# A two-layer graph network: another order of its beginning, and of all engines' queues

## The chip, the cores and the metric

The kernel runs on one core of a Trainium2 chip. The metric is the device time in microseconds; the number before is the median of ten runs. Five engines work side by side, each through its own queue of instructions: PE (matrix products), DVE (vector), ACT (scalar functions), POOL, and SP, which here only issues transfers. ACT and POOL issue transfers as well. An instruction waits on semaphores for what it needs, and what stands behind it in the same queue waits with it.

## The reference

x and adj are 64 graphs of 256 nodes with 256 features and a 256 x 256 adjacency, in float32.

```python
# layer 0
deg = adj.sum(-1); deg = where(deg != 0, deg, 1)
a = deg^-0.5 * adj * deg^-0.5 + max(alpha, 1e-10) * I
x = layernorm(x + (a @ x) @ W.T + b)
# layer 1, on the x of layer 0
xc = x transposed                                # channels x nodes
h = relu(bn1(conv1(xc)))                         # 1 tap
x_conv = relu(bn2(conv2(h)) + xc) transposed     # 17 taps, padding 8
s = x @ w_se.T + b_se                            # 3 columns
A = exp(-|s_n - s_m|^2) * adj
x_nmp = A @ relu(x @ w_msg.T + b_msg)
y = GRUCell(input [x_conv, x_nmp], hidden x)
out = layernorm(x + y)
```

## The kernel before, in words

The 64 graphs go through in four groups (q) of Q = 16. The convolution with 17 taps (conv2) is done in the frequency domain: every graph is cut into 8 tiles of 32 nodes, each tile with its margins (48 points) is transformed by a product with a small table (fwd, L442), the products over channels are done for each frequency with transformed weights (p_k, L497), and DVE carries out the inverse transform (real_transform, complex_begin, complex_end; L599 to L708). So a group has three stages: layer0 and layer1 for each graph, up to the transform (graphs, L866); the products and the inverse (products, complex_end); and the gates of the recurrent cell with the last layer norm (gru, L753). The stages of different groups are interleaved by generators: a stage yields after each piece, and merge, take and the table PLACES say whose piece is traced next (L835 to L877, L950 to L991). In the first group the pieces of weights (L270) stand beside the graphs: they scale the taps, transform them with a second table (dft_w, L283) and store them in DRAM (ud), from where the products read them again.

The queues are not written out by hand. The program is traced in an order, and the framework then simulates it with a model of how long instructions take and puts each engine's instructions into its queue in the order in which the simulation issues them, the earlier traced ahead of the later among those that are ready. The same simulation decides which buffer of a pool a tile gets.

The beginning is what most of the change is about. At L106 to L113 the loads of graphs 0 and 1 are asked for on SP (adj_t, then x_t, each 256 KB), with alpha between them, and the weights of layer 0, conv1 and the messages on ACT. Then come:

- batch_norms (L139): eight vectors are loaded as 16 rows (L144), transposed (L148), turned into a scale and a shift, and spread over all partitions by products of a matrix of ones with diagonals (L165). The scale of bn1 goes into wc1 (L167), its shift into bc1 (L170); that of bn2 is handed to weights.
- layer0 (L325): degrees (L334 by DVE for graphs 0 and 1, L337 by ACT for the others), their inverse roots (dis, L340, POOL), the transposed adjacency (p_adjT, L349; copied by ACT, L350), its two diagonal blocks with alpha added (adjT, L352, DVE), x scaled by dis (x1, L361, ACT) and x plus bias (L362, POOL). Then the first product (p_hT, L369), the second (p_out, L379), the sum (L383) and the layer norm (L294). It yields ahead of the first product, ahead of the second, and at its end.
- tables (L196): a row of cosines is written on one partition by 48 memsets (period, L199). w_row (L216, L217) and fwd_row (L240, L241) are filled by one copy for every frequency, real and imaginary. Both rows go through DRAM: w_row to wd and from there to the 85 partitions of wt (L220 to L224), from which dft_w is made (L231); fwd_row to fm, which POOL fills with zeros first (L210, L242), and from there in six shifted pieces to fwd (L246).
- At L879 to L888 these are traced in the order: vectors, first taps, biases, layer0 of graphs 0 and 1, the rest of the batch norms, the tables, the load of graph 2.

Of the kernel before, what the change touches and what calls it, by code (L numbers as in the profile page):

```python
# [9 lines left out]
F32 = mybir.dt.float32  # L10
# [4 lines left out]
P = 128  # L15
# [5 lines left out]
def bcast_rows(v, n, rows=P):  # L21

    return bass.AP(tensor=v.tensor, offset=v.offset, ap=[[0, rows], [1, n]])
# [3 lines left out]
def kernel(  # L27
# [41 lines left out]

    const = ctx.enter_context(tc.tile_pool(name="const", bufs=1))  # L70
# [18 lines left out]
    def load(g):  # L89
        if g >= B:  # L90
            return
        ain[g] = loads.tile([P, NCH, N], F32, name="adj_t")
        nc.sync.dma_start(ain[g], adj[g].rearrange("(c p) m -> p c m", p=P))
        xin[g] = loads.tile([P, NCH, D], F32, name="x_t")
        nc.sync.dma_start(xin[g], x[g].rearrange("(c p) f -> p c f", p=P))
# [9 lines left out]

    load(0)  # L106
    nc.sync.dma_start(alpha_t, bcast_rows(alpha, 1))
    load(1)
    nc.scalar.dma_start(w0, w0T.rearrange("(k p) o -> p k o", p=P))
    nc.scalar.dma_start(b0_t, bcast_rows(b0, D))  # L110
    nc.scalar.dma_start(wc1[:, :, :D], conv1T.rearrange("(k p) o -> p k o", p=P))
    nc.scalar.dma_start(wc1[:, :, D:], w_seT.rearrange("(k p) o -> p k o", p=P))
    nc.scalar.dma_start(wmsg, w_msgT.rearrange("(k p) o -> p k o", p=P))  # L113
# [4 lines left out]
    neg_half = const.tile([P, 4], F32)  # L118
    nc.vector.memset(neg_half, -0.5)
# [19 lines left out]
    def batch_norms(pool):  # L139


        vectors = pool.tile([16, P], F32, name="bn_in")
        for i, a in enumerate((bn1_g, bn2_g, bn1_b, bn2_b, bn1_m, bn2_m, bn1_v, bn2_v)):
            nc.sync.dma_start(vectors[2 * i : 2 * i + 2], a.rearrange("(c p) -> c p", p=P))  # L144
        scale = pool.tile([P, D], F32, name="scale")
        yield
# [41 lines left out]
    fm_rows = 2 * P + NT  # L188
    fm0 = P - PAD
    fm = dram.tile([fm_rows, FL], F32, name="fm")  # L190
# [5 lines left out]
    def tables(pool):  # L196
        period = pool.tile([1, 25 * FL], F32, name="period")
# [10 lines left out]
        zeros = pool.tile([NT, FL * fm_rows // NT], F32, name="zeros")  # L208
        nc.gpsimd.memset(zeros, 0.0)
        nc.gpsimd.dma_start(fm.rearrange("(p r) f -> p (r f)", p=NT), zeros)  # L210

        for r in range(2):
            nc.vector.memset(w_row[:, :, r, NF], (0.5, 1.0)[r])
        nc.vector.memset(w_row[:, 1::2, 1, NF], 0.0)
        for n, f in enumerate(FREQ):
            nc.vector.tensor_copy(w_row[:, :, 0, n], wave(f, False, TAPS))  # L216
            nc.vector.tensor_copy(w_row[:, :, 1, n], wave(f, True, TAPS))  # L217

        wd = dram.tile([TAPS, 2 * NU], F32, name="wd")
        nc.sync.dma_start(wd.unsqueeze(0), w_row.rearrange("p t h n -> p t (h n)"))  # L220
        wt = pool.tile([KT, 2 * NU], F32, name="wt")
        for c in range(GC):
            nc.sync.dma_start(wt[c * TR : (c + 1) * TR], wd[:TR])
        nc.sync.dma_start(wt[GC * TR :], bcast_rows(wd[TR], 2 * NU, GC))  # L224
# [10 lines left out]

        for r in range(2):
            nc.vector.memset(fwd_row[:, :, 2 * r], 1.0)
        nc.vector.memset(fwd_row[:, 1::2, 2], -1.0)
        for n, f in enumerate(FREQ):
            nc.vector.tensor_copy(fwd_row[:, :, RE[n]], wave(f, False, FL))  # L240
            nc.vector.tensor_copy(fwd_row[:, :, IM[n]], wave(-f, True, FL))  # L241
        nc.sync.dma_start(fm[fm0 : fm0 + FL].unsqueeze(0), fwd_row)  # L242
        for j in range(GT // 2 + 2):

            first = fm0 + PAD - NT * (j - 1)
            nc.sync.dma_start(fwd[:, j, :], fm[first : first + P])  # L246
# [75 lines left out]
    ADJT, DIS, XB, X1, XN, MSG, AT = {}, {}, {}, {}, {}, {}, {}  # L322


    def layer0(g):  # L325
# [7 lines left out]
        if g < 2:  # L333
            nc.vector.tensor_reduce(deg, a_t, AX.X, ALU.add)  # L334
        else:
            for c in range(NCH):
                nc.scalar.activation(adjT[:, c, 0:2, :].rearrange("p n q -> p (n q)"), a_t[:, c, :], AF.Copy, accum_out=deg[:, c : c + 1])  # L337
# [12 lines left out]
        nc.scalar.copy(adjT[:, :, 0:3:2, :], p.rearrange("p c (n q) -> p c n q", q=P))  # L350
        for mc in range(NCH):
            nc.vector.scalar_tensor_tensor(  # L352
                adjT[:, mc, 1, :], ident, adeg[:, mc : mc + 1], adjT[:, mc, 2 * mc, :],
                op0=ALU.mult, op1=ALU.add,
            )
# [4 lines left out]
        for c in range(NCH):  # L360
            nc.scalar.activation(x1[:, c, :], x_t[:, c, :], AF.Copy, scale=dis[:, c : c + 1])  # L361
# [497 lines left out]
    def run(stage):  # L859
        for _ in stage:  # L860
            pass
# [17 lines left out]
    with tc.tile_pool(name="setup", bufs=1) as setup:  # L879
        norms = batch_norms(setup)  # L880
        next(norms)
        load_taps(setup, 0)
        nc.sync.dma_start(bmsg_t, bcast_rows(b_msg, D))
        nc.sync.dma_start(bc1[:, D:], bcast_rows(b_se, NSE))
        run(merge(layer0(0), layer0(1)))
        scale2 = next(norms)
        tables(setup)
        load(2)  # L888

# [155 lines left out]
```

## Time and profile before

| | |
|---|---|
| median of ten runs | 2192.78 us (2190.47 to 2200.57) |
| the profiled execution | 2195.79 us |
| its span, first to last instruction | 2194.0 us |
| granted clock of PE, mean | 0.984 |
| PE idle in the first 60 us | 60 - 35.64 = 24.4 us |
| PE idle from 400 to 520 us | 120 - 98.15 = 21.9 us |
| DMA, mean over the span | 139 GB/s |

The 40 slices of the span, in tenths of busy time (54.85 us each; PEclk is the clock granted to PE):

```profile
PE   5999989969999997999999998899999999899998
PEld 4878778758888886888888887688888887678887
DVE  5555558875568799655556889855555879987666
ACT  3556533445441122456542122446553112222222
POOL 2444310113321234223222224322231223344442
PEclk9999999979999999999999999999999999999999
DMA  3756656443347644333336654433333654444441
```

A row is one engine, a digit one slice. PE is at 9 in most slices; it is below in the first, and in those where DVE is at 8 or 9 and the stages of two groups meet. A product of 256 columns takes about 0.22 us of PE when they follow each other (24 of p_rz in 5.18 us on the chain), so busy PE is work that the order of the queues can't remove.

### The profile page before, as it was taken

The numbers are of one execution on the slowest core, as the hardware profiler recorded it, in microseconds if no ns is written. First come the engines' busy times: TensorE is split into PE (matmuls) and PEld (weight loads), VectorE is DVE, ScalarE is ACT, GpSimd is POOL, SyncE is SP. The second block draws the span as 40 slices with busy tenths as digits, with TensorE's granted clock in tenths as the row PEclk, the third lists the DMA queues.
The fourth block names the chain that finished last, engine by engine and source line by source line (L and its number), as shares of the span: only waits on it lengthen the run. The fifth ranks groups of instructions, "written<-read, shape, count | busy, mean of one in ns | idle before, by whom it ended". The sixth has DMA issues, their size and how long they took to land. (4 is left out here: it accounts for less than half of the span.)

```text
span 2194.0 us, 28939 instructions
## 1 busy us (share of the span) xinstructions
PE 2067.6 (94%) x9805; PEld 1751.9 (80%) x9805; DVE 1553.6 (71%) x3743; ACT 828.8 (38%) x1838; POOL 664.1 (30%) x641
## 2 busy tenths in 40 slices
PE   5999989969999997999999998899999999899998
PEld 4878778758888886888888887688888887678887
DVE  5555558875568799655556889855555879987666
ACT  3556533445441122456542122446553112222222
POOL 2444310113321234223222224322231223344442
PEclk9999999979999999999999999999999999999999
DMA  3756656443347644333336654433333654444441
GB/s 98 231 187 199 221 164 217 154 140 112 100 114 217 199 118 125 115 101 111 109 108 177 206 159 123 127 106 115 102 97 120 203 163 117 119 120 111 104 113 54
DMA packets 251822, 305.83 MB, mean 139 GB/s; under 512 B 18796, under 2 KB 230336, under 8 KB 251673
## 3 DMA queue, kind: packets, MB, share of 16 engines
q1 hardware_dynamic: 183338, 199.93, 30.0%
q10 hardware_dynamic: 45280, 68.04, 8.8%
q0 software_dynamic: 23056, 36.01, 8.4%
q8 instruction: 78, 1.28, 0.2%
q14 instruction: 70, 0.57, 0.1%
HBM read 200.79 MB, written 103.12 MB: 139 GB/s over the span
## 5 line engine op out<-in xcount | busy, mean ns | idle before, releaser
L767 PE MATMUL p_rz<-wrz,sums 128*128 128x256 f32 x1536 | 356.0, 383 | 19.4 <-DVE gn L809 9.8
L804 PE MATMUL p_n<-wn,inputs 128*128 128x256 f32 x1536 | 351.3, 381 | 16.1 <-DVE first L780 15.7
L767 PEld LDWEIGHTS p_rz<-wrz,sums 128*128 128x128 f32 x1536 | 288.5, 191 | 70.9 <-issue 15.8
L804 PEld LDWEIGHTS p_n<-wn,inputs 128*128 128x128 f32 x1536 | 285.7, 190 | 62.1 <-DVE first L780 18.9
L767 PE MATMUL p_rz<-wrz,inputs 128*128 128x256 f32 x1152 | 272.9, 380 | 2.1 <-ACT inputs L739 1.5
L304 POOL TENSOR_TENSOR ln_rs<-ln_rs,neg_half 128x2 f32<-128x2 f32 x129 | 100.2, 777 | 539.8 <-DVE ln_rs L303 454.1
L767 PEld LDWEIGHTS p_rz<-wrz,inputs 128*128 128x128 f32 x1152 | 216.8, 190 | 33.7 <-ACT inputs L739 3.6
L340 POOL TENSOR_TENSOR dis<-deg,neg_half 128x2 f32<-128x2 f32 x64 | 48.5, 757 | 428.1 <-DVE deg L338 321.7
L816 ACT ACTIVATE nn<-gn 128x256 f32<-128x256 f32 x128 | 53.2, 416 | 325.0 <-DVE gn L813 324.3
L497 PE MATMUL p_k<-u,VM 128*128 128x256 f32 x736 | 175.2, 380 | 0.0
L314 ACT ACTIVATE x_g<-x_g,ln_mr,ln_rs 128x256 f32<-128x256 f32 x128 | 70.0, 593 | 256.4 <-DVE ln_mr L312 256.4
L497 PEld LDWEIGHTS p_k<-u,VM 128*128 128x128 f32 x736 | 138.6, 190 | 19.7 <-DMA u<-ud 0.9
L442 PE MATMUL p_dft<-fwd,h 128*128 128x240 f32 x512 | 121.4, 382 | 24.0 <-ACT h L411 23.1
L407 PE MATMUL p_conv<-wc,xn 128*128 128x259 f32 x512 | 128.6, 394 | 14.4 <-ACT xn L399 13.8
L748 POOL TENSOR_TENSOR sums<-inputs 128x384 f32<-128x384 f32 x64 | 69.4, 1085 | 230.1 <-issue 172.2
L369 PE MATMUL p_hT<-adjT,x 128*128 128x256 f32 x512 | 126.5, 392 | 8.3 <-DVE adjT L352 8.1
L442 PEld LDWEIGHTS p_dft<-fwd,h 128*128 128x128 f32 x512 | 98.0, 196 | 41.0 <-ACT h L411 32.7
L473 PE MATMUL p_nmp<-aT,msg 128*128 128x256 f32 x512 | 123.7, 385 | 2.6 <-DVE aT L468 2.6
L379 PE MATMUL p_out<-w,hT 128*128 128x256 f32 x512 | 124.2, 386 | 1.0 <-ACT hT L374 0.7
L407 PEld LDWEIGHTS p_conv<-wc,xn 128*128 128x128 f32 x512 | 97.5, 194 | 33.9 <-ACT xn L399 18.6
L428 PE MATMUL p_msg<-wmsg,xn 128*128 128x256 f32 x512 | 123.4, 385 | 0.0
L362 POOL TENSOR_TENSOR x_t<-x_t,b_t 128x512 f32<-128x512 f32 x64 | 84.7, 1324 | 128.0 <-ACT x L361 88.4
(153 smaller groups left out, 3845.5 us busy)
## 6 DMA issues: line engine op xcount, KB each, us to landing
u<-ud SPq DMA_DIRECT2D x284, 256.0 KB
xn_d<-xn ACTq DMA_DIRECT2D x64, 512.0 KB
inputs<-xn_d SPq DMA_DIRECT2D x64, 512.0 KB
ud<-u_set POOLq DMA_DIRECT2D x39, 480.0 KB, 6.1
adj_t<-in_adj_dram SPq DMA_DIRECT2D x64, 256.0 KB
x_t<-in_x_dram SPq DMA_DIRECT2D x64, 256.0 KB
x_d<-x ACTq DMA_DIRECT2D x64, 256.0 KB
x_g<-x_d SPq DMA_DIRECT2D x64, 256.0 KB
```

Of the source, the lines that this page charges most:

```text
L304: nc.gpsimd.tensor_tensor(rs[:, : len(chunks)], rs[:, : len(chunks)], neg_half[:, : len(chunks)], op=ALU.pow)
L314: nc.scalar.activation(y[:, c, :], y[:, c, :], AF.Identity, bias=mr[:, c : c + 1], scale=rs[:, c : c + 1])
L362: nc.gpsimd.tensor_tensor(x_t, x_t, b0_t.unsqueeze(1).to_broadcast([P, NCH, D]), op=ALU.add)
L369: nc.tensor.matmul(p[:, k, :], x1[:, mc, k * P : (k + 1) * P], adjT[:, mc, 1 - mc : 3 - mc, :].rearrange("p n q -> p (n q)"), start=mc == ...
L379: nc.tensor.matmul(p[:, c, :], hT[:, k, c * P : (c + 1) * P], w0[:, k, :], start=k == 0, stop=k == DCH - 1)
L407: nc.tensor.matmul(p, x1T[:, k, c * P : (c + 1) * P], wc1[:, k, :], start=k == 0, stop=k == DCH - 1)
L428: nc.tensor.matmul(p[:, c, :], x1T[:, k, c * P : (c + 1) * P], wmsg[:, k, :], start=k == 0, stop=k == DCH - 1)
L442: nc.tensor.matmul(p[:, t0 * FL : t1 * FL], h[:, c, k * P : (k + 1) * P], fwd[:, first : first + t1 - t0, :].rearrange("p t f -> p (t f)") ...
L473: nc.tensor.matmul(p[:, k, :], msg[:, mc, k * P : (k + 1) * P], aT[:, mc].rearrange("p n q -> p (n q)"), start=mc == 0, stop=mc == NCH - 1,)
L497: nc.tensor.matmul(p[:, j * D : (j + 1) * D], v[:, k, :], u[:, k, :], start=k == 0, stop=k == DCH - 1)
L767: nc.tensor.matmul(p[:, j * D : (j + 1) * D], a[:, k], wrz[:, b, k], start=k == 0, stop=k == HALF - 1)
L804: nc.tensor.matmul(p[:, o * D : (o + 1) * D], lhsT, w, start=j == 0, stop=j == len(part) - 1)
```

## The change

The first part rearranges the beginning. The bn vectors become a tile of the constants and their loads are issued ahead of most others, four on ACT and four on SP; alpha is asked for on ACT directly after graph 0; a small ACT copy into bc1 stands ahead of everything else on ACT's engine; the weights' loads move from ACT to SP, apart from w0. The tables are made with fewer copies (one for each frequency pair only for part of the frequencies, the others copied or negated from there in one operation each; w_row is copied from fwd_row) and go from SBUF to SBUF, so that wd, fm and the zeros go away, and fwd is cleared by POOL. `issue_after` puts the instructions of its block behind a named instruction on the same engine. Degrees of graphs 0 and 1 are taken by ACT. The order of tracing becomes: two pieces of layer0, the tables, two pieces, the batch norms, the rest of layer0.

The second part is one line: the whole kernel is put into a block that is scheduled with `schedule_with_timeline_sim=True`, so that the simulation which orders all queues and gives out the buffers uses another model.

```diff
--- before.py
+++ after.py
@@ -67,6 +67,8 @@
     NQ = B // Q
     assert N == 256 and D == 256 and B % Q == 0 and TAPS == FL - NT + 1 and FL == 3 * NT // 2
 
+
+    ctx.enter_context(tc.block(schedule_with_timeline_sim=True))
     const = ctx.enter_context(tc.tile_pool(name="const", bufs=1))
     dram = ctx.enter_context(tc.tile_pool(name="dram", bufs=1, space=bass.MemoryType.DRAM))
 
@@ -103,20 +105,25 @@
     bmsg_t = const.tile([P, D], F32)
     alpha_t = const.tile([P, 1], F32)
 
+    vectors = const.tile([16, P], F32, name="bn_in")
+    neg_half = const.tile([P, 4], F32)
+    nc.vector.memset(neg_half, -0.5)
     load(0)
-    nc.sync.dma_start(alpha_t, bcast_rows(alpha, 1))
+    nc.scalar.dma_start(alpha_t, bcast_rows(alpha, 1))
+
+    nc.scalar.copy(bc1[:, :4], neg_half)
+    for i, a in enumerate((bn1_g, bn2_g, bn1_b, bn2_b, bn1_m, bn2_m, bn1_v, bn2_v)):
+        (nc.sync if i % 2 else nc.scalar).dma_start(vectors[2 * i : 2 * i + 2], a.rearrange("(c p) -> c p", p=P))
+    nc.scalar.dma_start(w0, w0T.rearrange("(k p) o -> p k o", p=P))
     load(1)
-    nc.scalar.dma_start(w0, w0T.rearrange("(k p) o -> p k o", p=P))
-    nc.scalar.dma_start(b0_t, bcast_rows(b0, D))
-    nc.scalar.dma_start(wc1[:, :, :D], conv1T.rearrange("(k p) o -> p k o", p=P))
-    nc.scalar.dma_start(wc1[:, :, D:], w_seT.rearrange("(k p) o -> p k o", p=P))
-    nc.scalar.dma_start(wmsg, w_msgT.rearrange("(k p) o -> p k o", p=P))
+    nc.sync.dma_start(b0_t, bcast_rows(b0, D))
+    nc.sync.dma_start(wc1[:, :, :D], conv1T.rearrange("(k p) o -> p k o", p=P))
+    nc.sync.dma_start(wc1[:, :, D:], w_seT.rearrange("(k p) o -> p k o", p=P))
+    nc.sync.dma_start(bc1[:, D:], bcast_rows(b_se, NSE))
 
 
     ident = const.tile([P, P], F32)
     make_identity(nc, ident)
-    neg_half = const.tile([P, 4], F32)
-    nc.vector.memset(neg_half, -0.5)
     nc.vector.tensor_scalar(alpha_t, alpha_t, MIN_ALPHA, None, op0=ALU.max)
 
 
@@ -139,11 +146,7 @@
     def batch_norms(pool):
 
 
-        vectors = pool.tile([16, P], F32, name="bn_in")
-        for i, a in enumerate((bn1_g, bn2_g, bn1_b, bn2_b, bn1_m, bn2_m, bn1_v, bn2_v)):
-            nc.sync.dma_start(vectors[2 * i : 2 * i + 2], a.rearrange("(c p) -> c p", p=P))
         scale = pool.tile([P, D], F32, name="scale")
-        yield
         p = bank("p_bn")
         nc.tensor.transpose(p[:, :16], vectors, ident[:16, :16])
         cols = pool.tile([P, 4, 4], F32, name="bn")
@@ -185,15 +188,13 @@
     KT = GC * TAPS
     TR = 16
 
-    fm_rows = 2 * P + NT
-    fm0 = P - PAD
-    fm = dram.tile([fm_rows, FL], F32, name="fm")
 
     ud = [dram.tile([NU * GC, GW, D], F32, name=f"ud{i}") for i in range(3)]
     fwd = const.tile([P, GT // 2 + 2, FL], F32)
     DFT_W = {}
 
     def tables(pool):
+
         period = pool.tile([1, 25 * FL], F32, name="period")
         for k in range(FL):
             nc.vector.memset(period[:, k::FL], math.cos(2 * math.pi * k / FL))
@@ -205,23 +206,40 @@
 
         fwd_row = pool.tile([1, FL, FL], F32, name="fwd_row")
         w_row = pool.tile([1, TAPS, 2, NU], F32, name="w_row")
-        zeros = pool.tile([NT, FL * fm_rows // NT], F32, name="zeros")
-        nc.gpsimd.memset(zeros, 0.0)
-        nc.gpsimd.dma_start(fm.rearrange("(p r) f -> p (r f)", p=NT), zeros)
-
+        nc.gpsimd.memset(fwd, 0.0)
         for r in range(2):
-            nc.vector.memset(w_row[:, :, r, NF], (0.5, 1.0)[r])
-        nc.vector.memset(w_row[:, 1::2, 1, NF], 0.0)
+            nc.vector.memset(fwd_row[:, :, 2 * r], 1.0)
+        nc.vector.memset(fwd_row[:, 1::2, 2], -1.0)
         for n, f in enumerate(FREQ):
-            nc.vector.tensor_copy(w_row[:, :, 0, n], wave(f, False, TAPS))
-            nc.vector.tensor_copy(w_row[:, :, 1, n], wave(f, True, TAPS))
-
-        wd = dram.tile([TAPS, 2 * NU], F32, name="wd")
-        nc.sync.dma_start(wd.unsqueeze(0), w_row.rearrange("p t h n -> p t (h n)"))
+
+            if f < 0 or f % 3 == 0:
+                nc.vector.tensor_copy(fwd_row[:, :, RE[n]], wave(f, False, FL))
+                nc.vector.tensor_copy(fwd_row[:, :, IM[n]], wave(-f, True, FL))
+        parts = fwd_row[:, :, 16:].rearrange("p t (h n) -> p t h n", h=2)
+        nc.vector.tensor_copy(parts[:, 0::2, :, :8], parts[:, 0::2, :, 8:])
+        nc.vector.tensor_scalar(parts[:, 1::2, :, :8], parts[:, 1::2, :, 8:], -1.0, None, op0=ALU.mult)
+        with tc.issue_after(DIAGONAL[0]):
+
+            for r in range(2):
+                nc.vector.memset(w_row[:, :, r, NF], (0.5, 1.0)[r])
+            nc.vector.memset(w_row[:, 1::2, 1, NF], 0.0)
+            for n0, n1 in ((0, 1), (1, 2), (2, 3), (3, 7), (7, NF)):
+                nc.vector.tensor_copy(w_row[:, :, 0, n0:n1], fwd_row[:, :TAPS, RE[n0] : RE[n0] + n1 - n0])
+            for n0, n1 in ((0, 1), (1, 2), (2, 3), (3, 7), (7, NF)):
+                nc.vector.tensor_scalar(
+                    w_row[:, :, 1, n0:n1], fwd_row[:, :TAPS, IM[n0] : IM[n0] + n1 - n0], -1.0, None, op0=ALU.mult
+                )
+        for j in range(GT // 2 + 2):
+
+            first = NT * (j - 1) - PAD
+            lo, hi = max(first, 0), min(first + FL, P)
+            nc.sync.dma_start(fwd[lo:hi, j, :], fwd_row[:, lo - first : hi - first])
+
         wt = pool.tile([KT, 2 * NU], F32, name="wt")
+        row = w_row.rearrange("p t h n -> p t (h n)")
         for c in range(GC):
-            nc.sync.dma_start(wt[c * TR : (c + 1) * TR], wd[:TR])
-        nc.sync.dma_start(wt[GC * TR :], bcast_rows(wd[TR], 2 * NU, GC))
+            nc.sync.dma_start(wt[c * TR : (c + 1) * TR], row[:, :TR])
+            nc.sync.dma_start(wt[GC * TR + c : GC * TR + c + 1], row[:, TR])
         mask = pool.tile([KT, GC], F32, name="mask")
         dft_w = DFT_W[0] = pool.tile([KT, 2, NU, GC], F32, name="dft_w")
         nc.vector.tensor_reduce(
@@ -232,18 +250,6 @@
             dft_w.rearrange("p h n c -> p (h n) c"), wt.unsqueeze(2).to_broadcast([KT, 2 * NU, GC]),
             mask.unsqueeze(1).to_broadcast([KT, 2 * NU, GC]),
         )
-
-        for r in range(2):
-            nc.vector.memset(fwd_row[:, :, 2 * r], 1.0)
-        nc.vector.memset(fwd_row[:, 1::2, 2], -1.0)
-        for n, f in enumerate(FREQ):
-            nc.vector.tensor_copy(fwd_row[:, :, RE[n]], wave(f, False, FL))
-            nc.vector.tensor_copy(fwd_row[:, :, IM[n]], wave(-f, True, FL))
-        nc.sync.dma_start(fm[fm0 : fm0 + FL].unsqueeze(0), fwd_row)
-        for j in range(GT // 2 + 2):
-
-            first = fm0 + PAD - NT * (j - 1)
-            nc.sync.dma_start(fwd[:, j, :], fm[first : first + P])
 
     TAPS_OF = {}
 
@@ -319,7 +325,7 @@
     xc_d = [dram.tile([Q, N, D], F32, name=f"xc_d{q}") for q in range(NQ)]
     x1_d = [dram.tile([Q, N, D], F32, name=f"x1_d{q}") for q in range(NQ)]
     xn_d = [dram.tile([P, 2 * DCH, N], F32, name=f"xn_d{g}") for g in range(B)]
-    ADJT, DIS, XB, X1, XN, MSG, AT = {}, {}, {}, {}, {}, {}, {}
+    ADJT, X1, X_SCALED, DIAGONAL = {}, {}, {}, {}
 
 
     def layer0(g):
@@ -330,11 +336,19 @@
         ADJT[g] = adjT
 
         deg = small.tile([P, NCH], F32, name="deg")
-        if g < 2:
-            nc.vector.tensor_reduce(deg, a_t, AX.X, ALU.add)
+        def degrees():
+            for c in range(NCH):
+                nc.scalar.activation(
+                    adjT[:, c, 0:2, :].rearrange("p n q -> p (n q)"), a_t[:, c, :], AF.Copy,
+                    accum_out=deg[:, c : c + 1],
+                )
+
+        if g == 1:
+
+            with tc.issue_after(X_SCALED[0]):
+                degrees()
         else:
-            for c in range(NCH):
-                nc.scalar.activation(adjT[:, c, 0:2, :].rearrange("p n q -> p (n q)"), a_t[:, c, :], AF.Copy, accum_out=deg[:, c : c + 1])
+            degrees()
         nc.vector.scalar_tensor_tensor(deg, deg, 0.0, deg, op0=ALU.is_equal, op1=ALU.add)
         dis = small.tile([P, NCH], F32, name="dis")
         nc.gpsimd.tensor_tensor(dis, deg, neg_half[:, :NCH], op=ALU.pow)
@@ -347,18 +361,19 @@
         for mc in range(NCH):
             for c in range(NCH):
                 nc.tensor.transpose(p[:, mc, c * P : (c + 1) * P], a_t[:, c, mc * P : (mc + 1) * P], ident)
-        nc.scalar.copy(adjT[:, :, 0:3:2, :], p.rearrange("p c (n q) -> p c n q", q=P))
+        copied = nc.scalar.copy(adjT[:, :, 0:3:2, :], p.rearrange("p c (n q) -> p c n q", q=P))
         for mc in range(NCH):
-            nc.vector.scalar_tensor_tensor(
+            DIAGONAL[g] = nc.vector.scalar_tensor_tensor(
                 adjT[:, mc, 1, :], ident, adeg[:, mc : mc + 1], adjT[:, mc, 2 * mc, :],
                 op0=ALU.mult, op1=ALU.add,
-            )
+            ).ins
 
 
         x1 = work.tile([P, NCH, D], F32, name="x1")
         X1[g] = x1
-        for c in range(NCH):
-            nc.scalar.activation(x1[:, c, :], x_t[:, c, :], AF.Copy, scale=dis[:, c : c + 1])
+        with tc.issue_after(copied.ins) if g < 2 else ExitStack():
+            for c in range(NCH):
+                X_SCALED[g] = nc.scalar.activation(x1[:, c, :], x_t[:, c, :], AF.Copy, scale=dis[:, c : c + 1]).ins
         nc.gpsimd.tensor_tensor(x_t, x_t, b0_t.unsqueeze(1).to_broadcast([P, NCH, D]), op=ALU.add)
 
         yield
@@ -877,14 +892,15 @@
             yield from given["other"]
 
     with tc.tile_pool(name="setup", bufs=1) as setup:
-        norms = batch_norms(setup)
-        next(norms)
         load_taps(setup, 0)
+        nc.sync.dma_start(wmsg, w_msgT.rearrange("(k p) o -> p k o", p=P))
         nc.sync.dma_start(bmsg_t, bcast_rows(b_msg, D))
-        nc.sync.dma_start(bc1[:, D:], bcast_rows(b_se, NSE))
-        run(merge(layer0(0), layer0(1)))
-        scale2 = next(norms)
+        firsts = merge(layer0(0), layer0(1))
+        run(take(firsts, 2))
         tables(setup)
+        run(take(firsts, 2))
+        scale2 = next(batch_norms(setup))
+        run(firsts)
         load(2)
 
         def gate_weights():
```

## The prediction

> **What bounds the kernel now.** I read the page's busy time and slices first, then the busy time in twelve stretches cut at the visible dips of PE, then PE's waits of the worst stretches, and last the order of time of the beginning. Busy time, by engine:
>
> ```profile
> PE 2067.6 (94%) x9805; PEld 1751.9 (80%) x9805; DVE 1553.6 (71%) x3743; ACT 828.8 (38%) x1838; POOL 664.1 (30%) x641
> ```
>
> PE lacks 2194.0 - 2067.6 = 126.4 us, and that is all that an order of instructions can win, since no matmul is taken away. Where it lies (us from, to; length; busy time of each engine; granted clock; DMA share and rate):
>
> ```profile
> 0.00:60.00 60.00, 35.64 (x142) 28.29 (x143) 35.39 (x217) 18.32 (x40) 15.95 (x26) 0.94 0.35 99
> 60.00:200.00 140.00, 136.09 (x660) 112.16 (x660) 77.04 (x198) 84.66 (x196) 62.04 (x59) 0.99 0.68 212
> 200.00:300.00 100.00, 89.89 (x418) 71.97 (x416) 46.58 (x130) 53.51 (x127) 34.48 (x33) 0.95 0.55 177
> 400.00:520.00 120.00, 98.15 (x449) 77.91 (x448) 93.46 (x262) 57.97 (x131) 27.92 (x27) 0.90 0.41 124
> 800.00:910.00 110.00, 97.24 (x437) 80.80 (x436) 100.25 (x236) 36.75 (x80) 41.55 (x37) 0.95 0.43 122
> 910.00:1290.00 380.00, 376.48 (x1828) 322.21 (x1827) 244.83 (x587) 157.83 (x353) 99.69 (x100) 1.00 0.46 138
> ```
>
> The reader is to see three kinds of stage: the beginning (24.4 us idle of 60), stages in which PE is full (60 to 200, 910 to 1290), and crossings in which DVE is nearly full and PE starves (21.9 us idle in 400 to 520, 12.8 in 800 to 910; two more, 1290 to 1420 and 1790 to 1960, lack 15.6 and 18.1; the end after 1960 lacks 9.3). What PE waited for in the first 60 us (total, times, longest):
>
> ```profile
> PE p_adjT L349 <- DMA adj_t<-in_adj_dram: 8.6, 2, 4.4
> PE p_hT L369 <- DVE adjT L352: 7.6, 1, 7.6
> PE p_norm L165 <- DVE bn L156: 4.3, 1, 4.3
> PE p_u L283 <- DVE dft_w L231: 1.7, 1, 1.7
> ```
>
> In the order of time (start, duration) these waits come from the queues:
>
> ```profile
> 8.84 0.51 ACT L361 ACTIVATE x<-x_t,dis 128x256 f32<-128x256 f32 x1
> 12.16 3.08 DVE L216 COPY w_row<-period 1x17 f32<-1x17 f32 x1
> 12.72 2.49 POOL L362 TENSOR_TENSOR x_t<-x_t,b_t 128x512 f32<-128x512 f32 x2
> 18.00 0.59 DVE L352 SCALAR_TENSOR_TENSOR adjT<-ident,adeg,adjT 128x128 f32<-128x128 f32 x2
> 18.39 6.12 PE L369 MATMUL p_hT<-adjT,x 128*128 128x256 f32 x16 [7.62 <-DVE adjT L352]
> 38.11 2.02 PE L407 MATMUL p_conv<-wc,xn 128*128 128x259 f32 x8 [0.67 <-ACT xn L399]
> 41.38 0.41 DVE L231 TENSOR_TENSOR dft_w<-wt,mask 85x240 f32<-85x240 f32 x1
> ```
>
> The last input of p_hT other than the diagonal is x1, there at 8.84 + 0.51 = 9.35; the diagonal (L352) came at 18.00 because DVE's queue had the 46 table copies ahead of it.
>
> [...] after a wait of 9.56 us at 469.01 eight p_dft take 3.57 us, against 1.62 warm. [...] the 3.08 us copy above, against a median of 0.16, lies over POOL's additions. [...] here it is 1.28 us, at 6.67, behind x0's arrival and in front of the first x1. [...] the store of zeros took 2.6 us to land.
>
> **The change, part by part: the beginning.**
> (1) The w_row work is put behind the diagonal of graph 0, and fwd_row behind the first pieces of layer0. p_hT can start near 9.7 instead of 18.39: 8.7 us off the chain. Nothing else holds it: adeg was ready at 8.68, and alpha, which landed for 8.26, is now first in ACT's queue.
> (2) The table load goes ahead of the data (the small ACT copy into bc1). Degrees of graphs 0 and 1 move to ACT, about 4 x 0.6 us by the later L337 rows (0.41 + 0.19), graph 1's behind x1 of graph 0. I set both together at 0: 1.28 us won, 1.2 us of degrees of graph 0 added on the chain. Bounds -1.3 and +1.2.
> (3) Batch norms ahead of out0. Before, PE did only norms from 28.89 to 36.09, while x1 of graph 0 was normalised at 29.33 + 1.09 = 30.42 and waited for its transposes until 36.09: 5.6 us off the chain. It is not free: the same work now stands ahead of out0. On DVE it is some 16 instructions: nine small at 0.16, six diagonals at 0.28 and the 0.68 and 0.42 of wc and bc, 4.2 us, plus a pow of 1.01 and turns between PE and DVE for a pair of diagonal buffers, 0.5 each. Part lies beside layer0 of graph 1, whose adjacency landed only at 9.65. Cost: 2 at least, 8 at most; I take 4, about the DVE work.
> (4) Tables. DVE before: 48 memsets 2.3 us, 46 copies of w_row at a pitch of 0.083 = 3.8 plus the 3.1 caught by POOL, 46 of fwd_row at 0.115 = 5.3. After: the memsets, 30 copies at 0.115 and two of 384 elements (0.41 by the dft_w row, 240 elements), w_row in 10 operations at 0.16 to 0.41 (272 elements are the largest): 2.3 + 3.5 + 0.8 + 2.5 = 9.1, against 14.5. The DRAM legs (w_row to wd to wt, fwd_row to fm to fwd) and the zeros go; dft_w at 41.4 was ended by that leg and held p_u 1.7 us. I count the 1.7 and leave the DVE time as slack. On SP, 6 fwd and 10 wt issues (0.4 each, 6.4 us) now wait for the rows, where load(2) stands behind; it was at 38.69, so even issued at 25 it is earlier. The eight vector issues at 0.53 stand ahead of load(1) on SP and of w0 on ACT, four on each: graph 1's adjacency up to 2 us later, beside graph 0's work.
> Sum: 8.7 + 5.6 + 1.7 - 4 = 12.0 us earlier at p_conv and p_u. From 60 to 200 PE is full, so the gain is carried on. A single-partition source for the SBUF-to-SBUF tables has no row in this trace: at worst it takes 6 us of the gain (as much as the old path with its two hops seems to have cost), at best nothing. Range of this part: -16 to -5.
>
> **The change, part by part: the queues.** The whole kernel is put into a block whose instructions are listed by simulating with another model. Instructions, sizes and counts stay; the order in each queue and the buffer that a tile gets may change. No view shows the new order. What bounds it: waits of PE after 60 us that lie outside the DVE-full crossings come to 3.9 + 10.1 + 0.9 + 3.5 + 3.5 + 2.5 = 24.4 us (the stretches 60 to 400, 520 to 800, 910 to 1290, 1420 to 1790). Those a better order could take; the 68 us in the crossings it can hardly take, DVE being full there. On the other side a poorer order can open new stalls, up to two as below (44 us). I take -4, a sixth of the 24.4: p_dft behind h, and p_n behind first, are waits of the kind where something ready stands behind something that isn't. [...]
>
> Against the profiled execution (2195.79 us, 1.8 of it outside the span): 2195.8 - 12 - 4 = 2179.8. The median shown is 2192.78, 3.0 lower: 2176.8, so 2177.
>
> **Rivals.**
> A, the forecast: 2177; own range 2160 to 2188.
> B, the beginning's gain is absorbed: something later than the first graphs sets the time, for instance the hand-over at 255 to 300, where the setup pool closes and u, stored by POOL, is read back. For it: 10.1 us idle there. Against it: PE is full from 60 to 255, and the weights' stores follow PE. Time: 2192.
> C, slower: the new order opens another cold stall at a crossing. Price, from the one at 459 to 490: waits of 9.6 + 5.3 us, then eight p_dft 3.57 for 1.62, eight p_hT 3.78 for 1.89, p_dist and p_out likewise, 5.6 us to 485.5 and some 7 in all: 22 us. One such: 2181 (the beginning alone) + 22 = 2203; two: 2225. It decides from the point where PE's idle time outside the first 60 us grows by more than the beginning's 12. For it: three other crossings with DVE full, whose stalls today are short (3.9 us at most), and turns of the stages written out in the program (PLACES and the takes), which don't move when the queues do. Against it: PE's priorities remain those of the program.
> D, the other model gives the same order: 2181, only the beginning shows.
>
> **How the numbers follow.** A 0.54, D 0.05, B 0.11, C 0.30. This kernel can be told from no change at about 0.2% (4.4 us: 2188.4 to 2197.2). A's tail gives 0.01 to that: faster 0.58, same 0.12, slower 0.30. The range takes A, D, B and one stall of C: 2155 (a queue gain of 24 with the 12) to 2215 (one stall and the beginning at its least, or a stall and a half). Outside lie C's two stalls, 0.13, and 0.05 below. Faster and slower both hold much; A's own range is given above.
>
> **What would show it.** Right: p_hT near 10 and p_conv near 26 instead of 38.11; PE idle in the first 60 us near 12; no wait of dft_w on wt; p_rows and p_dft at the first crossing as long as before. (1) is wrong if L352 of graph 0 still ends after 12. (3) is wrong if out0 stands idle behind the norms for over 8 us. The forecast is wrong if PE's idle time in the four crossings leaves 68 us by more than 10, to either side, or the clock there falls.

## The result, and the profile after

| | before | after |
|---|---|---|
| median | 2193.8 us (beside the runs of after) | 2298.87 us (2292.54 to 2303.79) |
| ratio | | 1.0472, 95% interval 1.0459 to 1.0485 |
| span of the profiled execution | 2194.0 us | 2293.3 us |
| granted clock of PE, mean | 0.984 | 0.965 |

The changed kernel is slower by 4.7%, some 104 us. The forecast, 2177 us with a range up to 2215, was wrong in its sign. The page of after, busy time by engine:

```profile
PE 2108.2 (92%) x9805; PEld 1782.9 (78%) x9805; DVE 1566.3 (68%) x3691; ACT 833.4 (36%) x1847; POOL 668.8 (29%) x640
```

PE does the same 9805 matmuls, yet is busy for 2108.2 us, 40.6 more than before, and idle for 2293.3 - 2108.2 = 185.1, 58.7 more: together the 99.3 us between the spans. So two fifths of the loss are matmuls at a lower clock (0.965 in the mean, for 0.984), and the rest is waiting. Where, by the same stretches as before (us from, to; length; busy time and instructions of PE, PEld, DVE, ACT, POOL; clock; DMA share and rate):

```profile
0.00:60.00 60.00, 43.23 (x152) 32.89 (x153) 33.99 (x163) 22.62 (x50) 22.30 (x31) 0.83 0.67 191
60.00:200.00 140.00, 121.00 (x546) 98.46 (x546) 77.01 (x157) 70.33 (x159) 64.29 (x61) 0.93 0.70 218
400.00:520.00 120.00, 95.83 (x432) 76.24 (x431) 91.07 (x256) 55.46 (x124) 25.10 (x24) 0.93 0.43 130
800.00:910.00 110.00, 89.92 (x370) 74.62 (x369) 108.20 (x230) 20.16 (x41) 40.39 (x28) 0.91 0.37 108
910.00:1290.00 380.00, 363.07 (x1747) 306.81 (x1746) 221.72 (x573) 168.98 (x383) 98.50 (x104) 0.98 0.41 120
1420.00:1790.00 370.00, 346.70 (x1648) 292.45 (x1647) 218.28 (x578) 166.43 (x372) 96.47 (x100) 0.98 0.34 103
```

The last of these looked so before:

```profile
1420.00:1790.00 370.00, 367.47 (x1785) 313.74 (x1784) 234.40 (x570) 155.09 (x345) 93.07 (x93) 1.00 0.44 131
```

The beginning does a little more work in its 60 us than before (152 matmuls for 142), at a lower clock (0.83 for 0.94). For its length, the largest loss is from 60 to 200, a stage in which PE had been full: 136.09 us busy before, 121.00 now, with 546 matmuls done for 660. From 910 to 1290 and from 1420 to 1790, full as well before, 13 and 21 us are gone. (The later stretches are shifted by the time already lost, so they show where PE starves, not the exact loss of a stage.) PE's waits over the whole run (total, times, longest):

```profile
PE p_conv L422 <- ACT xn L414: 42.1, 40, 6.7
PE p_n L819 <- DVE trz L796: 22.1, 5, 6.6
PE p_n L819 <- DVE first L795: 20.1, 8, 5.7
PE p_u L289 <- DVE taps L281: 11.4, 4, 4.5
...
PE p_dft L457 <- ACT h L426: 6.0, 5, 2.5
```

Before, the longest in total were these:

```profile
PE p_dft L442 <- ACT h L411: 23.1, 10, 9.6
PE p_n L804 <- DVE first L780: 15.7, 13, 2.4
PE p_conv L407 <- ACT xn L399: 13.8, 11, 3.9
```

So the waits of p_conv, of p_n and of p_u grow, and that of p_dft for h gets shorter. From 60 to 200 us two of them make nearly all of PE's idle time (19.0 us, 3.9 before): p_u waits 8.0 us for its taps, and p_conv 10.9 us for xn. The first, in the order of time (start, duration):

```profile
83.63 7.15 PE L289 MATMUL p_u<-taps,dft_w 85*120 85x256 f32 x16 [4.46 <-DVE taps L281]
90.57 2.67 PE L457 MATMUL p_dft<-fwd,h 128*128 128x240 f32 x8
```

The pieces of the weights now come earlier and in clumps of 16 products, and PE waits for DVE, which has to scale their taps; then the matmuls are slow (16 of p_u take 3.62 us elsewhere, eight of p_dft 1.78). The second, late in the first group:

```profile
119.95 3.69 PE L289 MATMUL p_u<-taps,dft_w 85*120 85x256 f32 x16 [1.85 <-DVE taps L281]
...
138.24 0.60 PE L413 MATMUL p_x1T<-ident,x 128*128 128x128 f32 x4
145.53 3.82 PE L422 MATMUL p_conv<-wc,xn 128*128 128x259 f32 x8 [6.69 <-ACT xn L414]
149.14 1.06 PE L363 MATMUL p_adjT<-ident,adj_t 128*128 128x128 f32 x4
```

Before, the same place looks so:

```profile
142.71 0.60 PE L398 MATMUL p_x1T<-ident,x 128*128 128x128 f32 x4
143.15 1.89 PE L283 MATMUL p_u<-taps,dft_w 85*120 85x256 f32 x8
144.88 1.92 PE L407 MATMUL p_conv<-wc,xn 128*128 128x259 f32 x8
```

There one piece of the weights (p_u), which needs nothing of the graph, stands between the transposes of x and the convolution and fills the turn over ACT. After the change p_conv stands directly behind p_x1T: 6.69 us of waiting, and then eight matmuls in 3.82 us for 1.92 (granted clock 0.50 from 145.5 to 149.2; before, 1.00 from 145.0 to 146.6). The tile's own view (count, ns, first and last start) shows the same:

```profile
L289 PE MATMUL p_u<-taps,dft_w x208: 377/379/753, 26.8 to 136.3; 85*120 85x256 f32 x104
```

The weights are through at 136 us; before, they were spread from 41.8 to 251.4. From there to the end of the group's graphs no piece of them is left to fill the turns: from 136 to 326 us p_conv waits for xn 13 times, 15.4 us in total, against 3 times and 2.1 us before.

### The profile page after: what moved, and what is told of

It reads as the page before. It is cut to its first block, busy times and chain, and to the rows that moved or that the text cites. A ratio compares the mean times of both kernels' runs of the same rounds, so it can differ in the third digit from the quotient of the medians.

```text
span 2293.3 us, 28979 instructions
## 1 busy us (share of the span) xinstructions
PE 2108.2 (92%) x9805; PEld 1782.9 (78%) x9805; DVE 1566.3 (68%) x3691; ACT 833.4 (36%) x1847; POOL 668.8 (29%) x640
## 5 line engine op out<-in xcount | busy, mean ns | idle before, releaser
L819 PE MATMUL p_n<-wn,inputs 128*128 128x256 f32 x1536 | 373.6, 396 | 52.2 <-DVE trz L796 22.1
L819 PEld LDWEIGHTS p_n<-wn,inputs 128*128 128x128 f32 x1536 | 300.3, 199 | 106.0 <-DVE trz L796 24.1
L782 PE MATMUL p_rz<-wrz,inputs 128*128 128x256 f32 x1152 | 282.6, 382 | 4.2 <-DVE trz L796 4.2
L310 POOL TENSOR_TENSOR ln_rs<-ln_rs,neg_half 128x2 f32<-128x2 f32 x129 | 122.0, 981 | 427.7 <-DVE ln_rs L309 400.9
L422 PE MATMUL p_conv<-wc,xn 128*128 128x259 f32 x512 | 136.8, 413 | 42.1 <-ACT xn L414 42.1
L763 POOL TENSOR_TENSOR sums<-inputs 128x384 f32<-128x384 f32 x64 | 86.0, 1343 | 269.5 <-issue 204.4
L394 PE MATMUL p_out<-w,hT 128*128 128x256 f32 x512 | 132.0, 403 | 16.6 <-ACT hT L389 9.3
L394 PEld LDWEIGHTS p_out<-w,hT 128*128 128x128 f32 x512 | 98.6, 199 | 41.2 <-ACT hT L389 20.2
L741 POOL DMA_DIRECT2D xc_g<-x_d x64 | 78.5, 1261 | 161.1 <-DMA xc_g<-xc_d 117.5
L457 PE MATMUL p_dft<-fwd,h 128*128 128x240 f32 x512 | 116.7, 372 | 6.2 <-ACT h L426 6.0
```

What stands on the lines that cost most here:

```text
L310: nc.gpsimd.tensor_tensor(rs[:, : len(chunks)], rs[:, : len(chunks)], neg_half[:, : len(chunks)], op=ALU.pow)
L394: nc.tensor.matmul(p[:, c, :], hT[:, k, c * P : (c + 1) * P], w0[:, k, :], start=k == 0, stop=k == DCH - 1)
L422: nc.tensor.matmul(p, x1T[:, k, c * P : (c + 1) * P], wc1[:, k, :], start=k == 0, stop=k == DCH - 1)
L457: nc.tensor.matmul(p[:, t0 * FL : t1 * FL], h[:, c, k * P : (k + 1) * P], fwd[:, first : first + t1 - t0, :].rearrange("p t f -> p (t f)") ...
L741: nc.gpsimd.dma_start(CONV[g], x1_d[g // Q][g % Q].rearrange("(c p) d -> p c d", p=P), accum_op=ALU.add)
L763: nc.gpsimd.tensor_tensor(S[:, 2], A11, A21, op=ALU.subtract)
```

## The experiments

The first pair splits the change. **The new beginning without the block line:**

```diff
-    ctx.enter_context(tc.block(schedule_with_timeline_sim=True))
```

> The changed kernel without its one line on the block: the new beginning under the old model. Theory 'queues' (the whole loss comes from the order that the other model gives, and the beginning is worth the 12 us forecast): about 2194 - 12 = 2182 us, the interval below 1.0. Rival 'beginning' (the later loads, the norms ahead of out0 or the single-partition tables cost, and the order only repeats it): near the 2299 of the whole change, at least above 2240. Rival 'absorbed': 2190 to 2196, the first p_conv earlier than 38 us but the end of the first group's graphs not.

2188.14 us, ratio 0.9968 (0.9959 to 0.9976): faster by 7.0 us, less than the 12 expected. **The block line alone, on the kernel before:**

```diff
+    ctx.enter_context(tc.block(schedule_with_timeline_sim=True))
```

> The kernel before with only the line on the block: the old beginning, all queues by the other model. Theory 'queues': the loss of the whole change and the beginning's gain on top of it, 2299 + 12 = 2311 us; PE's idle time outside the first 60 us grows by some 70 us or more, and p_u ends near 140 us instead of 251. Rival 'beginning': 2190 to 2200. If both parts cost, the two runs share the 105 us between them.

2299.99 us, ratio 1.0485 (1.0455 to 1.0516). The line alone makes the whole loss, some 106 us. PE's idle time behind the first 60 us grows by 69 us, as expected, and p_u ends at 152 us, somewhat later than expected; the time stays under the 2311 of the expectation, since under the line the beginning's gain doesn't show (2299.99 without it, 2298.87 with it). How far each kernel is when a given matmul ends (us, counted in the traces of one execution each; those of before and of the beginning alone differ by 9.8 us, their medians by less):

| | before | beginning alone | line alone | after | after less beginning alone |
|---|---|---|---|---|---|
| 128th p_nmp: graphs of group 0 end | 302.1 | 292.8 | 333.3 | 326.0 | 33.2 |
| 290th p_k: products of group 1 begin | 655.8 | 646.3 | 695.2 | 685.4 | 39.1 |
| 570th p_k: the same, group 2 | 1176.3 | 1166.6 | 1240.3 | 1236.0 | 69.4 |
| 850th p_k: the same, group 3 | 1695.1 | 1685.4 | 1785.4 | 1783.7 | 98.3 |
| 1536th p_n, the last: near the end | 2184.7 | 2175.0 | 2285.7 | 2284.6 | 109.6 |

No single stall makes the loss: 33 us come with the graphs of group 0, some 30 with each of the two stretches from one group's products to the next, and 11 after the last of them.

The line does three things: it orders each engine's queue, SP's among them, and it gives out buffers. The next kernels keep it, and put single queues back into the order that the beginning alone has, by ordering edges without a semaphore between neighbours of one queue (in the traces, the queues that were put back run in exactly that order, by line and tile):

```diff
+    def queue_order(engine, packed):
+        queued = [i for i in nc.cur_bb.bb.instructions if i.engine == engine]
...
+        for before, behind in zip(order, order[1:]):
+            tc.add_manual_dep(
+                queued[behind], queued[before].name,
+                mybir.DependencyInfo(mybir.DependencyClass.NoSync, mybir.DependencyReason.DATA), reason="queue order",
+            )
...
+    queue_order(mybir.EngineType.PE, """...""")
```

**PE's queue put back:**

> The changed kernel, other model, but PE's queue put into exactly the order that the old model gives it (the order of the run with the new beginning alone); the other queues are ordered by the other model around it. Theory 'run-ahead on PE' (the other model lets work that depends on little, the weights' p_u and the gates' p_rz and p_n, pass ahead of the graphs' chain in PE's queue, and the later graphs have nothing left to fill their waits): at least 80 of the 111 us between 2188 and 2299 come back, so 2185 to 2219; p_u ends near 245 us again and PE's waits for xn fall from 42 us to under 15. Rival 'DVE' (DVE's order is what costs: vector work of the transform and gates ahead of what PE waits for): 2260 or more.

2248.16 us, ratio 1.0249 (1.0231 to 1.0268). It wins 49 us of the 111 that lie between after and the beginning alone, fewer than expected and more than the rival allows: neither holds. p_conv's wait for xn falls under 15 us, as expected, and another wait grows:

```profile
PE p_dft L457 <- ACT h L426: 46.9, 28, 5.6
...
PE p_conv L422 <- ACT xn L414: 7.3, 9, 1.8
```

**DVE's queue put back:**

> The changed kernel, other model, with DVE's queue alone in the old order. Theory 'run-ahead on PE': PE's order stays mostly the other model's, so most of the loss stays, 2250 to 2300. Rival 'DVE': 2185 to 2220. If both queues recover it, the two orders hang together and either is enough.

2264.27 us, 1.0320 (1.0291 to 1.0349): 33 us, within the band of the run-ahead, and too little for the rival "DVE". **PE, DVE, ACT and POOL put back,** with SP and the buffers left to the other model:

> The changed kernel, other model, with the queues of PE, DVE, ACT and POOL all in the old order; SP's transfers and the buffers that tiles get are left to the other model. Theory 'queues': 2182 to 2195, as the new beginning alone (2188). If the buffers or SP's order cost: above 2210.

2186.81 us, 0.9961 (0.9950 to 0.9971), the time of the beginning alone, as expected. The queues' orders of these engines carry the whole loss; with them put back, SP's order and the buffers cost nothing that shows. The reverse, **the beginning alone with PE's queue in the order of after:**

> The reverse: the new beginning under the old model, with PE's queue in exactly the order of the changed kernel, the other queues ordered by the old model around it. Theory 'run-ahead on PE': 2270 to 2310. Rival 'DVE': 2190 to 2230.

2343.90 us, 1.0683 (1.0659 to 1.0708): above both expectations, and worse than after itself. Its PE waits:

```profile
PE p_conv L421 <- ACT xn L413: 52.5, 41, 6.2
PE p_xcT L751 <- DMA xc_g<-x_d: 41.2, 5, 30.0
```

The first is the wait of after, made by PE's order alone. The second is new: PE's queue asks for the gates' transposes at a time at which the other queues, in their own order, haven't yet brought the data. Here the order of one queue doesn't fit the orders of the others.

**PE and DVE put back:**

> The changed kernel, other model, with PE's and DVE's queues both in the old order; ACT, POOL and SP by the other model around them. Old order on PE alone brought back 51 of the 111 us between 2188 and 2299, on DVE alone 35. Theory 'two queues' (each of the two feeds the other, and both orders are needed): 2185 to 2200. Rival 'ACT and POOL' (what is left after PE sits in the scalar and POOL queues): 2210 or more.

2218.34 us, 1.0107 (1.0075 to 1.0139): the expectation that these two are all of it fails, and the rival holds. **PE, DVE and ACT put back:**

> The changed kernel with the queues of PE, DVE and ACT in the order that the new beginning has under the old model; POOL, SP and the buffers left to the other model. With PE and DVE so ordered the ratio was 1.0107, with POOL too 0.9961: some 31 us lie in the orders of ACT and POOL. Theory 'ACT': there PE waited 48.0 us for h of the batch norm (23.1 before), and ACT's sigmoids of the gates waited 65.3 us for DVE, 25.2 under the old order: h stands behind sigmoids that aren't ready. Then this run is at 2182 to 2196 and PE's wait of p_dft for h falls below 30. Rival 'POOL' (its additions for the gates stand ahead of the powers of the layer norms): 2206 to 2220, h above 40.

2188.68 us, 0.9963 (0.9948 to 0.9977): ACT it is, and POOL's order costs nothing that shows. The waits of PE and ACT for p_dft and for the sigmoids, with PE and DVE put back:

```profile
PE p_dft L457 <- ACT h L426: 48.0, 29, 9.6
...
ACT trz L804 <- DVE trz L802: 65.3, 27, 5.7
```

and with ACT put back too:

```profile
PE p_dft L457 <- ACT h L426: 23.4, 11, 9.6
...
ACT trz L804 <- DVE trz L802: 25.0, 20, 2.4
```

The sigmoids are only a part of the reason. With PE and DVE put back, p_dft waits 15 times for over 1 us. In two of these (6.7 and 8.2 us) a sigmoid that waited for DVE stands shortly ahead of the last step of h in ACT's queue; in eleven (1.3 to 2.0 us) it is nn of the gates, and mostly the layer norm of x ahead of it, that waited for DVE. So, put back in this sequence, PE's order gives 49 us, DVE's 31, ACT's 32 and POOL's under 1: differences of the ratios, times 2193.

Each queue that is put back takes away other waits of PE. Its idle time just before four of its products (us in total):

| | before | after | PE put back | PE, DVE | PE, DVE, ACT | weights in turn (below) |
|---|---|---|---|---|---|---|
| p_conv, mostly for ACT | 14.4 | 42.1 | 7.4 | 6.2 | 7.9 | 35.5 |
| p_n, for DVE | 16.1 | 52.2 | 54.5 | 19.3 | 20.9 | 50.3 |
| p_dft, for ACT | 24.0 | 6.2 | 46.9 | 48.1 | 23.4 | 13.1 |
| p_u, mostly for DVE | 1.7 | 14.5 | 0.0 | 2.2 | 2.2 | 0.4 |

The wait that ACT's order mends, p_dft for h, is short in after itself; it appears only once PE's queue is put back.

Then which work moved. **The weights' pieces held in their turn:** their PE and DVE instructions may not pass what was traced on that engine before their piece began. The rest of the program is that of after, and the other model orders its queues anew.

```diff
+    def in_turn(stage):
...
+            for i in list(traced[start:]):
+                if i.engine in last:
+                    tc.add_manual_dep(
+                        i, last[i.engine].name,
+                        mybir.DependencyInfo(mybir.DependencyClass.NoSync, mybir.DependencyReason.DATA), reason="in turn",
+                    )
...
-    others = [weights(setup, i, scale2) for i in range(NPARTS)]
+    others = [in_turn(weights(setup, i, scale2)) for i in range(NPARTS)]
```

> The changed kernel, other model, with one restriction: PE and DVE instructions of a weights piece may not pass ahead of what was traced before them on their engine. Theory 'run-ahead' (work that waits for little is let ahead of the graphs and is missing later as filler): the first group's graphs end near 300 us instead of 326 and p_u is spread to 250 us, total 2299 - 25 = 2274 (2265 to 2282), the later groups losing as much as before. Rival 'not the run-ahead' (p_conv behind its own transposes and the like cost, whoever fills): 2290 or more.

2267.39 us, 1.0331 (1.0298 to 1.0363): 31 us back, as expected. The tile's view of this kernel:

```profile
L289 PE MATMUL p_u<-taps,dft_w x208: 377/379/477, 36.3 to 250.0; 85*120 85x256 f32 x104
```

Its pieces reach to 250.0 again, no product of theirs is over 477 ns, and the 128th p_nmp ends at 302.4 for 326.0. By the table above it is p_u's own waits for its taps that go, and with them the stall of 6.69 us and 15 us of busy time (2093.2 for 2108.2); p_conv still waits 35.5 us, though never over 1.7. So this run shows what the run-ahead of the weights costs, and not that the missing filler alone costs it.

**The gates held in the same way as well,** those of the last group apart:

```diff
-    early = gates(q, range(EARLY))
+    early = in_turn(gates(q, range(EARLY)))
...
-    late = gates(q, range(EARLY, Q))
+    late = in_turn(gates(q, range(EARLY, Q)))
```

> The same restriction for the gates of all groups as well. Theory 'run-ahead': it is the gates that run ahead in groups 1 to 3, so most of the rest comes back: 2190 to 2225. Rival: above 2250, since f_pe_old_order with every matmul in the old place still stood at 2248 for want of DVE's order.

2304.90 us, 1.0495 (1.0468 to 1.0522): a miss, 36 us slower than with the weights alone. The waits of PE:

```profile
PE p_n L819 <- DVE first L795: 44.8, 5, 12.6
PE p_dft L457 <- ACT h L426: 33.6, 21, 3.5
```

The sums that p_n needs (first, DVE) are late. **The gates held on PE alone:**

> As weights_in_turn (PE's and DVE's instructions of the weights' pieces may not pass what was traced ahead of them; 1.0331), and the gates held in turn as well, but on PE alone. With the gates held on PE and DVE the ratio was 1.0495, with PE's longest wait that of p_n for the sums on DVE. Theory 'DVE': holding the gates' vector work made it late, and with DVE free of it the gates' matmuls in turn win: 2225 to 2262. Rival 'PE': a gate's matmul held in its turn stands in PE's queue ahead of work that is ready, whatever DVE does: 2285 or more. Between them neither decides.

2265.85 us, 1.0323 (1.0301 to 1.0345), between the two theories and equal to the weights alone: holding the gates' matmuls wins nothing (p_conv's waits fall from 35.5 us to 20.8, and p_dft's rise from 13.1 to 35.2), and holding their vector work as well costs the 36 us. That fits the queues as they were: counted in the two programs, on DVE 38.6% of the instructions pass something traced earlier even under the old model, so the traced order was never DVE's order. On PE it was: 1.2% of its 5351 queued instructions pass anything, against 21.7% under the other model, by 14.5 places in the mean over all and by 356 at most.

Last, a term of the beginning. **Batch norms behind out0 again,** in the beginning alone:

```diff
-        run(take(firsts, 2))
-        scale2 = next(batch_norms(setup))
         run(firsts)
+        scale2 = next(batch_norms(setup))
```

> The new beginning under the old model, with the batch norms behind out0 of both graphs again instead of ahead of it; all else of the beginning stays. By my forecast's step (norms ahead of out0: 5.6 us won, 4 given back) it is 1.6 us later at p_conv, near 32.1 instead of 30.5, and 1.6 us longer: 2188 to 2191 against 2187. Rival: the move is worth nothing or costs, since p_hT to p_conv took 19.7 us before and 19.9 with the norms moved: p_conv at 29 to 31 and no difference that the rounds show. Second rival: it is worth the whole 5.6: p_conv near 36 and 2192.

2188.55 us, 0.9964 (0.9950 to 0.9977): no difference from the beginning alone, as the first rival has it. The order of time of this kernel:

```profile
10.68 5.81 PE L383 MATMUL p_hT<-adjT,x 128*128 128x256 f32 x16 [1.45 <-ACT adjT L363]
...
25.45 3.12 PE L167 MATMUL p_norm<-diagonal,ones 128*128 128x128 f32 x10 [4.34 <-DVE bn L158]
...
30.52 3.82 PE L421 MATMUL p_conv<-wc,xn 128*128 128x259 f32 x8 [0.68 <-ACT xn L413]
```

and that of the beginning alone:

```profile
10.61 3.44 PE L383 MATMUL p_hT<-adjT,x 128*128 128x256 f32 x8 [1.37 <-ACT adjT L363]
...
21.18 1.06 PE L393 MATMUL p_out<-w,hT 128*128 128x256 f32 x2
...
30.49 3.69 PE L421 MATMUL p_conv<-wc,xn 128*128 128x259 f32 x8 [0.68 <-ACT xn L413]
35.92 2.27 PE L288 MATMUL p_u<-taps,dft_w 85*120 85x256 f32 x8 [1.74 <-DVE dft_w L248]
```

p_conv starts at 30.5 either way.

## Why the prediction was wrong

**The step that failed is the queues' term, -4 us; it is +106** (the line alone; 1.0485 of 2193). Three of its arguments fell.

- "Those a better order could take", and its reverse, that a poorer one opens "up to two" new stalls of 22 us: I had taken the idle time outside the crossings, 24.4 us, as what is at stake, and PE's busy time as fixed. Both moved: 58.7 us more idle time, and 40.6 us more for the same matmuls. A full PE only shows that the present order fills it. From 60 to 200 us it was full with a piece of p_u between the products of the graphs; with these run ahead, the same stage loses 15 us. An order can also lose the turns that filler covers now, which no idle time shows, and the time for which the filler itself isn't ready. The price of one cold stall was of the right kind (6.69 us of wait, then 1.9 us of slow matmuls); the number of waits was not, with 40 of p_conv for xn alone.
- "PE's priorities remain those of the program", against rival C: under the other model a fifth of PE's instructions pass earlier ones. The expectation that these priorities hold was not read from any view, and it decided between A and C.
- "p_dft behind h, and p_n behind first" as waits that a better order takes: right for the first alone, which falls from 23.1 us to 6.0, more than the whole term. It is outweighed by p_n (16.1 to 52.2), p_conv (14.4 to 42.1) and p_u (1.7 to 14.5). That one order would trade one wait for others had no place in the sum.

Rival C was right in its sign and in what kills the gain, PE's idle time growing by more than the beginning wins; it was priced at 2203 or 2225. It sat at the crossings, and the loss does not: the table of how far each kernel is has 33 us in the graphs of group 0 alone. So one sign named for a wrong forecast, PE's idle time in the four crossings, hardly moves (73.2 us in the same stretches, for 68.4); the other, a lower clock there, shows in three of them (800 to 910: 0.91 for 0.95; 1290 to 1420: 0.96 for 0.97; 1790 to 1960: 0.96 for 1.00). One reading behind that price was off: eight p_dft at a granted clock of 1.00 take 1.78 us by the view (after, from 151.92; 1.62 is the distance from their start to that of the next product).

**The beginning's term, -12 us, was right in mechanism and too large**: -7.0 (-9.0 to -5.3) without the line, inside its range of -16 to -5.

- (1) The diagonal behind the table copies: right. It ends at 10.12 + 0.60 = 10.72 instead of 18.59, and p_hT starts at 10.61, 7.8 us earlier (8.7 forecast).
- (3) The norms, +5.6 - 4 = 1.6 won: nothing at p_conv, which starts at 30.49 with them ahead and at 30.52 with them behind. Out0 starts 4.8 us behind p_hT's end, the cost that I took as 4, and the gain at p_conv was that same time and no more.
- A term that was missing: PE's clock. From 30 to 40 us the granted clock was 0.70, 0.83 before, and p_conv took 3.69 us for 2.02, 1.8 times as long. So p_conv starts 7.6 us earlier and ends only 40.1 - 34.2 = 5.9 earlier. Why the clock fell here is not shown: from 20 to 40 us PE is idle for 5.0 us, and 5.7 before.
- (4) "No wait of dft_w on wt": p_u waits 1.74 us for dft_w, as long as before. The prediction had put this wait down to the leg through DRAM, and the record speaks against it:

```profile
35.16 0.17 DVE L434 TENSOR_SCALAR scols<-nsq 128x4 f32<-128x4 f32 x1
35.46 0.41 DVE L248 TENSOR_TENSOR dft_w<-wt,mask 85x240 f32<-85x240 f32 x1
```

On DVE, dft_w stands directly behind the last of the steps that follow p_conv. Before it was so as well: that step ended at 41.28, and dft_w started at 41.38. SP issued the last piece of wt by 33.83 here, and by 31.61 with the norms late; dft_w starts at 35.46 and 35.69, no earlier for the earlier pieces. So its place in DVE's queue is the likelier cause; no run moved it alone.
- B, that the gain is absorbed, is refuted: the lead of the beginning alone is 5.9 us at the first p_u, 9.3 at the end of group 0's graphs and 9.7 near the end. Why it grows was not tried.

What stays open: the run-ahead of the weights is 31 us of the 111 between after and the beginning alone, shown by holding them; how much of it is their own waiting, and how much the missing filler, is not separated. The rest, some 80 us, is shown to lie in the joint orders of PE, DVE and ACT; which pieces carry it is only indicated by the waits for trz, first, xn and h. The run-ahead of the gates' matmuls on PE costs nothing in total, once the weights are held. The fastest kernels tried are the beginning without the line and its three equals, at 0.996 to 0.997 of the time before.

## What to carry to other kernels

A stage in which an engine is full is not safe from a new order: look for what fills its turns, and price a reordering by the turns that would be bare without the filler, and by what the filler waits for when it comes too early. One wait that a new order shortens says nothing of the sum: here p_dft's got shorter by 17 us, and p_n's longer by 36. An option that reorders all queues should be tried by itself, since its gain or loss (here 106 us) hides that of the edit beside it (7 us). Queue orders have to fit each other: putting back one of them recovered only a part here, and one queue of the other order among three of the old was worse than all in the other (2344 us against 2299).

## What the runs showed of the hardware

More idle time of PE came with slower matmuls, at no fixed price, so its busy time is no fixed amount of work: after has 58.7 us more idle time than before, and its same 9805 matmuls take 40.6 us more; with DVE's queue put back (span 65.3 us longer than before, clock 0.980) it is 50.0 more and 15.3 more.

Matmuls stayed slow for over 8 us of work after a wait. After the wait of 4.46 us shown above, PE works without a break from 83.63 us on; the clock granted from 84 to 92 us was 0.50, and from 93 to 95 us it was 1.00.

SP took 0.50 to 0.59 us (beginning alone) to issue each transfer of wt from a row on one partition, and 0.56 to 0.76 (after) for fwd, where I had counted 0.4: 9.8 us for the sixteen, instead of 6.4.
